# A graph-attention kernel: no repeated blocks at the ends of the spans, k and q[dst] in one PSUM tile, one load of edge features a step

## The chip, the cores and the metric

The kernel runs on one core of one Trainium2 chip. The metric is device microseconds (us) of one execution; the time before is the median of ten runs. TensorE is called PE in the profile, VectorE DVE, ScalarE ACT, GpSimd POOL and SyncE SP.

## The reference, cut to what matters

One layer of graph attention over N = 12500 nodes and E = 212500 edges of F = 128 features, with 8 heads of 16. The edges come sorted by their destination `dst`.

```python
h  = relu(layernorm(x))
q  = h @ Wq.T + bq;   v = h @ Wv.T + bv          # per node
k  = edge_attr @ Wk.T + bk                        # per edge
in_m, out_m, diag_m = sum16(q[src]*k), sum16(q[dst]*k), sum16(q[src]*q[dst])   # 8 heads each
score = (segsoftmax(in_m/4, dst) + segsoftmax(out_m/4, dst) + segsoftmax(diag_m/4, dst)) * edge_weight
out = x + leaky_relu(segsum(score * v[dst], dst) @ Wo.T + bo, 0.1)
```

So each edge has 24 logits, a softmax runs over all edges that end in one node, and two sums per node (the denominators and the weighted numerators) are all that goes back to the nodes.

## The kernel before, in words

All of the work is in `ordered_path`; `general_path` is skipped by a branch for these inputs.

**Blocks, spans and steps.** The edges are cut into NB = 416 blocks of BE = 512 (the last has EL = 20 edges). There are S = 5 spans of G = 83 blocks, and 5 x 83 + 1 = 416. A step t works on block t of each span, and there are T = G + 1 = 84 steps, so g = 5 t + s runs over 420 blocks: step 83 does the first block of spans 1 to 4 a second time (it needs their first edges, because a node's edges may reach over the end of a span), and the block of 20 edges, whose rest is filled with zeros.

**Preparation** (to about 130 us): weights and biases are turned, q of all nodes is computed and written to `q_table` (fp32) and `q3_table` (three bf16 terms), the sorted destinations become `rel_d` (place of the edge's node in its block) and `far_d` (minus 1e30 where a new node begins). The first LOOK = 9 blocks are gathered on POOL, and AHEAD = 6 blocks of edge features are loaded.

**The work on one block g**, by helper:

- `gather(g)` (L647): four indirect DMAs on POOL, 128 rows of q[src] each, into `qq[:, :, 0, :]`; the pool `gath` has QQ = 11 buffers of 4 KB per partition. Gather j of block g + LOOK also waits for a product of iteration g on PE (`behind`), which is a pacing rule only.
- `fetch_edges(g)` (L636): one 256 KB load of the block's edge features on the SP queue, six blocks ahead.
- `turn(g)` (L1100): four PE transposes of the features into PSUM `eT_ps` (L1103), copied by ACT to `eT` (L1105).
- `one_hots(g)` (L1092): two ACT passes (L1097, L1098) that make the one-hot matrix `oh` of the block's destinations.
- `spread_q(g)` (L1118): four PE products of `oh` with the window of q rows give q[dst] in PSUM `qd_ps` (2 buffers; L1122); ACT copies it to `qq[:, :, 1, :]` (L1124).
- `project(g)` (L1109): the bias (L1111) and four fp32 products `eT` x `wk` (L1113) give k in PSUM `k_ps` (2 buffers).
- `logits(g)` (L1128): on DVE the 512-wide product q[src] * q[dst] (L1133), the 1024-wide product of both halves of `qq` with k (L1134) and the reduction to 24 logits (L1136) in `lT`.

**The work on a step**, spread over the five iterations of later steps: `turn_logits` (l_ps, L1149) and `scan_on` at s = 0, `scan_back` at s = 1, `turn_max` (m_ps, L1175) and `powers` (L1181, exp L1182) at s = 2, `show_ends` (d_ps L1203, sel L1206, L1207) and `weigh_powers` (L1189) at s = 3, `to_rows` (w_ps L1216, rows L1221) and `put_rows` (five small stores) at s = 4. `fetch(t + 2)` and `fetch_rows(t + 2)` load `relb`, `far` and `win` on SP at s = 3. `nodes_before` and `nodes_between` do the finished nodes, four tiles every second step: two h passes each at s = 2 and 3 on ACT (L1014), two transposes and copies `hT` (L1034, L1037), the products with wv and wo (L1040, L1042), a slope pass (L1061), maximum and sum (L1066, L1067), and the store (L1073). Nodes at the ends of spans (`rest`) wait for the end: their sums come back by `ends_ab` loads (L1004 on SP, L1006 on the ACT queue), then scores, products and stores.

**The order is written by hand.** `pin` chains the instructions of each engine (and each DMA queue) in the order in which the code issues them. In the main loop (L1309) iteration g issues

```python
spread_q(g + 1); project(g + 1); turn(g + 2); logits(g); one_hots(g + 3)
# then the step's helper of this s, then nodes_between
```

so ACT's order in one iteration is: copy of q[dst] (g+1), copy of eT (g+2), the two one-hot passes (g+3), then what the step and the nodes need; PE's is: spread (g+1), bias and products (g+1), transposes (g+2), then the step's products.

Of the kernel before, what the change touches and what calls it, by code (L numbers as in the profile page):

```python
# [17 lines left out]
DIM = 16  # L18
# [454 lines left out]
def ordered_path(ctx: ExitStack, tc: tile.TileContext, flag, x, src, dst, edge_attr, edge_weight,  # L473
# [108 lines left out]
    LOOK, QQ, AHEAD, EA = 9, 11, 6, 7  # L582
# [28 lines left out]
    def fetch(t):  # L611

        if t >= T:
            return
        at, part = block_rows(t)
        relb = load.tile([K3, S, BE], BF, name="relb")
        pin(nc.sync.dma_start(relb, rel_d[part].rearrange("(s b) e -> s b e", b=G)
                              [None, :, at, :].to_broadcast([K3, S, BE])))
        far = load.tile([R, BE + 1], BF, name="far", bufs=4)
        for s in range(S):  # L620
            lo = (s * G + t) * BE
            pin(nc.sync.dma_start(far[s * H3:(s + 1) * H3, :],
                                  far_d[None, lo:lo + BE + 1].to_broadcast([H3, BE + 1])))
        _, base_v[t] = nc.values_load_multi_w_load_instructions(
            bases[0:1, t, 0:S], engines=[mybir.EngineType.SP], min_val=0, max_val=N - 1,
            skip_runtime_bounds_check_because="the indices of nodes are below N")
        st[t] = dict(relb=relb, far=far)

    def fetch_rows(t):
        if t >= T:  # L630
            return
        win = st[t]["win"] = load.tile([K3, S, F], BF, name="win")
        for s in range(S):
            pin(nc.sync.dma_start(win[:, s, :], q3_table[bass.ds(base_v[t][s] * 3, K3), :]))

    def fetch_edges(g):  # L636
        if g < S * T:
            ea = load.tile([P, JN * F], F32, name="ea", bufs=EA)
            b0 = (g % S * G + g // S) * BE
            n = min(BE, E - b0)  # L640
            if n < BE:
                nc.vector.memset(ea, 0.0)
            pin(nc.sync.dma_start(ea[:n // JN, :],
                                  edge_attr[b0:b0 + n, :].rearrange("(p j) f -> p (j f)", j=JN)))
            eas[g] = ea

    def gather(g):  # L647
        if g < S * T:
            qq = gath.tile([P, JN, 2, F], F32, name="qq")
            for j in range(JN):  # L650
                rows = pin(nc.gpsimd.indirect_dma_start(  # L651
                    out=qq[:, j, 0, :], out_offset=None, in_=q_table,
                    in_offset=bass.IndirectOffsetOnAxis(
                        ap=src_i[:, g % S * G + g // S, j:j + 1], axis=0)))
                if (g - LOOK, j) in behind:
                    tc.add_manual_dep(rows.ins, behind[g - LOOK, j], mybir.DependencyInfo(
                        mybir.DependencyClass.Sync, mybir.DependencyReason.SCHED_ONLY),
                        reason="close behind the products")
            qqs[g] = qq

# [14 lines left out]
    with tc.tile_pool(name="prep", bufs=1) as prep, \  # L675
# [234 lines left out]
        for g in range(-2, GN):  # L910
            if g + 2 < GN:
                rectify(g + 2)
            if 0 <= g + 1 < GN:
                turn_h(g + 1)
            if g >= 0:
                nodes_q(g)
            ready(g + 4)
            measure(g + 6 + min(max(g, 0), 6))
            if g in side:
                side[g]()  # L920
            if 9 <= g < 9 + AHEAD:
                fetch_edges(g - 9)
        for g in range(LOOK):
            gather(g)
        edges_4()
# [160 lines left out]
    with tc.tile_pool(name="work", bufs=2) as work, \  # L1086
            tc.tile_pool(name="scan", bufs=2) as scan, \
            tc.tile_pool(name="ps", bufs=1, space=PSUM) as ps:
        ks, eTs, qds, ohs, lTs = {}, {}, {}, {}, {}
        end = S * T  # L1090
# [9 lines left out]
        def turn(g):  # L1100
            eT_ps = ps.tile([P, JN, P], F32, name="eT_ps", bufs=1)
            for j in range(JN):
                pin(nc.tensor.transpose(eT_ps[:, j, :], eas[g][:, j * F:(j + 1) * F], ident))  # L1103
            eT = work.tile([P, JN, P], F32, name="eT", bufs=3)
            pin(nc.scalar.copy(eT, eT_ps))  # L1105
            eTs[g] = eT
            del eas[g]

        def project(g):  # L1109
            k_ps = ps.tile([P, JN, F], F32, name="k_ps", bufs=2)  # L1110
            pin(nc.tensor.matmul(k_ps, ones3, bk3, start=True, stop=False))  # L1111
            for j in range(JN):
                pin(nc.tensor.matmul(k_ps[:, j, :], eTs[g][:, j, :], wk, start=False,  # L1113
                                     stop=(j == JN - 1)))
            ks[g] = k_ps
            del eTs[g]

        def spread_q(g):  # L1118
            s, d = g % S, st[g // S]
            qd_ps = ps.tile([P, JN, F], F32, name="qd_ps", bufs=2)  # L1120
            for j in range(JN):
                pin(nc.tensor.matmul(qd_ps[:, j, :], ohs[g][:, j * P:(j + 1) * P],  # L1122
                                     d["win"][:, s, :], start=(j == 0), stop=(j == JN - 1)))
            pin(nc.scalar.copy(qqs[g][:, :, 1, :], qd_ps))  # L1124
            qds[g] = qd_ps
            del ohs[g]

        def logits(g):  # L1128
            s, t = g % S, g // S
            if s == 0:  # L1130
                lTs[t] = scan.tile([P, JN, S, H3], F32, name="lT", bufs=4)
            prod = work.tile([P, JN, 3, F], F32, name="prod")
            pin(nc.vector.tensor_mul(prod[:, :, 2, :], qqs[g][:, :, 0, :], qds[g]))  # L1133
            pin(nc.vector.tensor_mul(prod[:, :, 0:2, :], qqs[g],  # L1134
                                     ks[g][:, :, None, :].to_broadcast([P, JN, 2, F])))
# [3 lines left out]
            del ks[g], qds[g], qqs[g]  # L1139
# [5 lines left out]

        def turn_logits(t):
            l_ps = small([R, P, JN], "l_ps")
            for j in range(JN):
                pin(nc.tensor.transpose(l_ps[:, :, j], lTs[t][:, j].rearrange("p s c -> p (s c)"),  # L1149
                                        ident))  # L1150
            st[t]["l"] = l_ps

        def scan_on(t):
            d = st[t]
            u = d["u"] = scan.tile([R, BE], F32, name="u", bufs=3)
            pin(nc.vector.tensor_tensor_scan(u, d["far"][:, :BE], d["l"].rearrange("r p j -> r (p j)"),  # L1156
# [7 lines left out]
        def scan_back(t):  # L1164
            d = st[t]
            m = d["m"] = scan.tile([R, BE], F32, name="m")
            pin(nc.vector.tensor_tensor_scan(m[:, ::-1], d["far"][:, BE:0:-1], d["u"][:, ::-1],  # L1167
                                             d["head"][:, 0:1] if t < T - 1 else -FAR,
                                             op0=ALU.add, op1=ALU.max))

        def turn_max(t):
            d = st[t]
            m_ps = d["mT"] = small([P, JN, R], "m_ps")
            for j in range(JN):
                pin(nc.tensor.transpose(m_ps[:, j, :], d["m"][:, j:BE:JN], ident[:R, :R]))  # L1175

        def powers(t):
            d = st[t]
            back = d["back"] = work.tile([P, JN, S, 2, H3], F32, name="back")
            e = back[:, :, :, 0, :]  # L1180
            pin(nc.vector.tensor_sub(e, lTs[t], d["mT"].rearrange("p j (s c) -> p j s c", s=S)))  # L1181
            pin(nc.scalar.activation(e, e, AF.Exp, scale=SCALE))  # L1182
            del lTs[t]

        def weigh_powers(t):
# [3 lines left out]
            pin(nc.vector.tensor_mul(back[:, :, :, 1, :], back[:, :, :, 0, :],  # L1189
                                     att.to_broadcast([P, JN, S, H3])))  # L1190
# [20 lines left out]
        def to_rows(t):  # L1211
            d = st[t]
            w_ps = small([3 * W, 2, 3, 2 * H3], "w_ps")
            for i, (lo, _) in enumerate(trios):
                for j in range(JN):
                    pin(nc.tensor.matmul(w_ps[:, i].rearrange("p s c -> p (s c)"),  # L1216
                                         d["sel"][:, j, lo:lo + 3, :].rearrange("p s w -> p (s w)"),
                                         d["back"][:, j, lo:lo + 3].rearrange("p s i c -> p (s i c)"),
# [53 lines left out]
        starts, holds = (0, 1, 3, 4, 6), ("eT_ps", "k_ps", "k_ps", "qd_ps", "qd_ps")  # L1272
# [3 lines left out]
        def spare():  # L1276
            return gath.tile([P, JN, 2, F], F32, name="qq").rearrange("p j i f -> p (j i f)")

        def halves():
            return spare().rearrange("p (i j f) -> i p j f", i=2, j=JN)  # L1280

        def begin_rest(at):
            if at in turned:
                late.update(zip(turned[at], halves()))
            for r, (of, begin) in enumerate(zip(rest, starts)):
# [8 lines left out]
                if at == LOOK + (3, 4, 7, 7, 7)[r]:  # L1294
                    of.held = ps.tile([P, JN, F], F32, name=holds[r], bufs=1 if r == 0 else 2)
# [13 lines left out]
        for g in range(end + 2 * S):  # L1309
            s, t = g % S, g // S  # L1310
            nodes_before(t, s)
            if g < end:
                gather(g + LOOK)
                fetch_edges(g + AHEAD)
# [10 lines left out]
            one_hots(g + 3)  # L1325
            if s == 0:
                later(turn_logits, t - 1)
                later(scan_on, t - 1)
                later(select, t - 2)
            elif s == 1:  # L1330
                later(scan_back, t - 2)
            elif s == 2:
                later(turn_max, t - 2)
                later(powers, t - 2)
            elif s == 3:
                later(show_ends, t - 2)
                later(weigh_powers, t - 2)
                fetch(t + 2)
                fetch_rows(t + 2)
            else:  # L1340
                later(to_rows, t - 2)
                later(put_rows, t - 2)
# [71 lines left out]
```

## Time and profile before

| what | value |
|---|---|
| median of 10 runs | 2323.13 us (2318.01 to 2326.63) |
| the profiled execution | 2319.08 us; span of its instructions 2317.2 us |
| mean granted TensorE clock | 0.786 |
| busy: DVE, PE, POOL, ACT | 1985.5, 1694.5, 1678.4, 1356.2 us (86, 73, 72, 59% of the span) |
| indirect DMAs on POOL | 1680, busy 1636.4 us, idle just before them 524.3 us |
| first and last of them start at | 82.0 and 2234.6 us |

Times in rows are microseconds from the start of the span, unless ns is written. Busy time of an engine counts what the profile shows of its instructions; the gap between two instructions of an engine is its idle time, put down to what ended it. The granted clock is the share of full speed that TensorE was given.

### The profile page before, as it was taken

The page shows a single profiled execution, that of the slowest core. Times are in us where ns is not written, and L with a number is a line of the kernel's source. Part 1 is how long each engine was busy: PE and PEld are TensorE (multiplying, and loading weights), DVE is VectorE, ACT ScalarE, POOL GpSimd, SP SyncE. Part 2 cuts the span into 40 slices and gives each one's busy share as a digit, 9 for nine tenths or more (in the row PEclk, how much of TensorE's full clock was granted, in tenths as well). Part 3 has the DMA queues.
Part 4 walks back from the last instruction along what each step waited for, and adds up shares of the span by engine and source line. Part 5 has one row for each costly group of instructions (what it writes and reads, how often), then busy time and mean ns, then how long its engine had stood idle before and what let it go on. Part 6 is the DMA issues. An engine that isn't in the chain of part 4 may idle for free.

```text
span 2317.2 us, 36525 instructions
## 1 busy us (share of the span) xinstructions
PE 1694.5 (73%) x10293; PEld 1350.2 (58%) x10293; DVE 1985.5 (86%) x2191; ACT 1356.2 (59%) x2462; POOL 1678.4 (72%) x1717
## 2 busy tenths in 40 slices
PE   6348878767777777777777877777787877677783
PEld 4236666555656566566556655656665656565562
DVE  7669999888888888888889898988888888898973
ACT  6647666556555656565656665665656556565651
POOL 4577777777777777777777777777777777777741
PEclk9658887777777778877877797787778779788876
DMA  6885555555455545554555565455545555565521
GB/s 198 265 255 171 170 164 142 152 144 145 130 149 161 148 135 162 152 151 131 162 158 143 145 171 148 134 155 156 147 139 169 146 149 142 144 169 142 164 57 54
DMA packets 326673, 354.48 MB, mean 153 GB/s; under 512 B 143655, under 2 KB 245376, under 8 KB 326152
## 3 DMA queue, kind: packets, MB, share of 16 engines
q1 hardware_dynamic: 257117, 235.44, 34.9%
q0 software_dynamic: 53920, 110.41, 18.2%
q10 hardware_dynamic: 15424, 6.19, 1.1%
q8 instruction: 85, 1.39, 0.2%
q14 instruction: 127, 1.04, 0.2%
HBM read 319.65 MB, written 32.17 MB: 152 GB/s over the span
## 4 chain that ended last, share of the span: by engine, by line
DMA 33%; PE 29%; DVE 17%; issue 11%; ACT 5%; POOL 4%; DVEq 0%; SPq 0%; POOLq 0%; ACTq 0%
DMA qq<-q_table,src_i 30%; PE k_ps L1113 10%; DVE prod L1134 6%; PE w_ps L1216 5%; POOL qq L651 4%; DVE prod L1133 4%; PE eT_ps L1103 4%; PE k_ps L1111 3%; PE node_ps L1042 2%; PE qd_ps L1122 1%; DMA q_table<-q 1%; ACT eT L1105 1%; ACT relb L1097 1%; PE d_ps L1203 1%; DVE u L1156 1%
## 5 line engine op out<-in xcount | busy, mean ns | idle before, releaser
L651 POOL DMA_INDIRECT qq<-q_table,src_i x1680 | 1636.4, 974 | 524.3 <-issue 242.0
L1136 DVE TENSOR_REDUCE lT<-prod 128x96 f32<-128x1536 f32 x420 | 736.2, 1753 | 14.3
L1113 PEld LDWEIGHTS k_ps<-wk,eT 128*128 128x128 f32 x3360 | 522.1, 237 | 292.0 <-issue 85.6
L1113 PE MATMUL k_ps<-wk,eT 128*128 128x128 f32 x3360 | 617.5, 340 | 14.3 <-ACT eT L1105 13.9
L1134 DVE TENSOR_TENSOR prod<-qq,k_ps 128x1024 f32<-128x1024 f32 x420 | 509.9, 1214 | 2.0 <-PE k_ps L1113 2.0
L1133 DVE TENSOR_TENSOR prod<-qq,qd_ps 128x512 f32<-128x512 f32 x420 | 286.6, 682 | 222.7 <-DMA qq<-q_table,src_i 187.2
L1105 ACT COPY eT<-eT_ps 128x512 f32<-128x512 f32 x420 | 245.9, 585 | 388.5 <-PE eT_ps L1103 369.4
L1122 PE MATMUL qd_ps<-win,oh 126*128 126x128 bf16 x1680 | 184.2, 239 | 319.9 <-DVE prod L1133 252.2
L1122 PEld LDWEIGHTS <-oh 126*128 126x128 bf16 x1680 | 143.5, 107 | 378.6 <-issue 302.4
L1103 PE MATMUL eT_ps<-ident,ea 128*128 128x128 f32 x1680 | 319.9, 325 | 1.0 <-DVE found L937 1.0
L1097 ACT ACTIVATE relb<-relb,before 126x512 bf16<-126x512 bf16 x420 | 304.4, 725 | 0.0
L1111 PE MATMUL k_ps<-b,ones 3*128 3x512 bf16 x420 | 185.2, 441 | 143.5 <-DVE prod L1134 142.5
L1098 ACT ACTIVATE oh<-relb 126x512 bf16<-126x512 bf16 x420 | 264.6, 630 | 18.8 <-issue 5.4
L1124 ACT COPY qq<-qd_ps 128x512 f32<-128x512 f32 x420 | 241.5, 575 | 49.1 <-PE qd_ps L1122 22.3
L1182 ACT ACTIVATE back<-back 128x480 f32<-128x480 f32 x84 | 50.7, 604 | 362.9 <-DVE back L1181 350.7
L1103 PEld LDWEIGHTS eT_ps<-ident,ea 128*128 128x128 f32 x1680 | 256.5, 173 | 1.3 <-DVE found L937 1.3
L1216 PE MATMUL w_ps<-back,sel 128*126 128x144 f32 x1344 | 215.4, 322 | 19.6 <-ACT sel L1207 10.0
L1216 PEld LDWEIGHTS w_ps<-back,sel 128*126 128x126 f32 x1344 | 207.3, 224 | 26.2 <-ACT sel L1207 21.8
L1175 PE MATMUL m_ps<-ident,m 120*128 120x120 f32 x336 | 72.3, 351 | 58.5 <-DVE m L1167 58.4
L1156 DVE TENSOR_TENSOR_SCAN u<-far,u,l_ps 120x512 f32<-120x512 bf16 x83 | 105.5, 1271 | 1.3 <-PE l_ps L1149 1.3
L1167 DVE TENSOR_TENSOR_SCAN m<-far,head,u 120x512 f32<-120x512 bf16 x83 | 105.9, 1276 | 0.0
L1175 PEld LDWEIGHTS m_ps<-ident,m 120*128 120x128 f32 x336 | 54.6, 217 | 75.9 <-DVE m L1167 72.4
(167 smaller groups left out, 1292.6 us busy)
## 6 DMA issues: line engine op xcount, KB each, us to landing
ea<-in_edge_attr_dram SPq DMA_DIRECT2D x419, 256.0 KB
relb<-rel_d SPq DMA_DIRECT2D x84, 630.0 KB
qq<-q_table,src_i POOLq DMA_INDIRECT x1680
win<-q_table SPq DMA_DIRECT2D x420, 31.5 KB
far<-far_d SPq DMA_DIRECT2D x420, 24.0 KB
q_table<-q SPq DMA_DIRECT2D x24, 384.0 KB
sums<-rows SPq DMA_DIRECT2D x412, 7.9 KB
q_table<-xq SPq DMA_DIRECT2D x24, 256.0 KB
```

The lines of the kernel that those rows point to most:

```text
L651: rows = pin(nc.gpsimd.indirect_dma_start(out=qq[:, j, 0, :], out_offset=None, in_=q_table, in_offset=bass.IndirectOffsetOnAxis(ap=src_i[: ...
L1097: pin(nc.scalar.activation(d, d, AF.Abs, bias=before[:K3]))
L1098: pin(nc.scalar.activation(oh, d, AF.Relu, bias=1.0, scale=-1.0))
L1103: pin(nc.tensor.transpose(eT_ps[:, j, :], eas[g][:, j * F:(j + 1) * F], ident))
L1105: pin(nc.scalar.copy(eT, eT_ps))
L1111: pin(nc.tensor.matmul(k_ps, ones3, bk3, start=True, stop=False))
L1113: pin(nc.tensor.matmul(k_ps[:, j, :], eTs[g][:, j, :], wk, start=False, stop=(j == JN - 1)))
L1122: pin(nc.tensor.matmul(qd_ps[:, j, :], ohs[g][:, j * P:(j + 1) * P], d["win"][:, s, :], start=(j == 0), stop=(j == JN - 1)))
L1133: pin(nc.vector.tensor_mul(prod[:, :, 2, :], qqs[g][:, :, 0, :], qds[g]))
L1134: pin(nc.vector.tensor_mul(prod[:, :, 0:2, :], qqs[g], ks[g][:, :, None, :].to_broadcast([P, JN, 2, F])))
L1136: pin(nc.vector.tensor_reduce(lTs[t][:, :, s, :], prod.rearrange("p j i (h d) -> p j (i h) d", d=DIM), AX.X, ALU.add))
L1216: pin(nc.tensor.matmul(w_ps[:, i].rearrange("p s c -> p (s c)"), d["sel"][:, j, lo:lo + 3, :].rearrange("p s w -> p (s w)"), d["back"][:, ...
```

## The change

- `end` becomes S * G = 415: the repeated blocks are not gathered, transposed or multiplied any more. The first 64 logits of each span's first block (`l_few`) are kept in `l_end` at step 1, moved up by one span with a small DMA; the 20 last edges are done once, as single edges, by `logits_few` in iteration s = 1 of step 1. Step 83 is left as a short one: scan, difference, exp and sums over 64 edges a span. It is done in the same five iterations as steps 81 and 82 (`now`), all after the last block.
- `qq` holds q[src] alone (2 KB per partition, 19 buffers), LOOK is 12. k and q[dst] get one PSUM tile `kq_ps` of two banks (2 buffers, as many banks as before); ACT copies its q[dst] half to a tile `qd` of its own. DVE multiplies q[src] with both halves (1024 wide), then `qd` with k (512 wide).
- `fetch_edges(t)` loads the features of a whole step (1.25 MB) into one of 2 buffers, one step ahead. `far` comes in one DMA instead of five.
- The loop has one iteration more after the blocks, and the tiles that `rest` borrows are named anew.

```diff
-    LOOK, QQ, AHEAD, EA = 9, 11, 6, 7
+    LOOK, QQ = 12, 19
+    end = S * G
...
-        for s in range(S):
-            lo = (s * G + t) * BE
-            pin(nc.sync.dma_start(far[s * H3:(s + 1) * H3, :],
-                                  far_d[None, lo:lo + BE + 1].to_broadcast([H3, BE + 1])))
+        lo = t * BE
+        of = bass.AP(far_d.tensor, far_d.offset + lo, [[G * BE, S], [0, H3], [1, BE + 1]])
+        pin(nc.sync.dma_start(far, of))
...
+    def fetch_edges(t):
+        if t < G:
+            ea = eas[t] = load.tile([P, S, JN * F], F32, name="ea")
+            pin(nc.sync.dma_start(
+                ea, edge_attr[:end * BE, :].rearrange("(s b p j) f -> p s b (j f)", s=S, b=G, p=P)
+                [:, :, t, :]))
...
         def project(g):
-            k_ps = ps.tile([P, JN, F], F32, name="k_ps", bufs=2)
+            k_ps = kqs[g][:, 0]
             pin(nc.tensor.matmul(k_ps, ones3, bk3, start=True, stop=False))
...
         def spread_q(g):
             s, d = g % S, st[g // S]
-            qd_ps = ps.tile([P, JN, F], F32, name="qd_ps", bufs=2)
+            kqs[g] = ps.tile([P, 2, JN, F], F32, name="kq_ps", bufs=2)
+            qd_ps = kqs[g][:, 1]
             for j in range(JN):
                 pin(nc.tensor.matmul(qd_ps[:, j, :], ohs[g][:, j * P:(j + 1) * P],
                                      d["win"][:, s, :], start=(j == 0), stop=(j == JN - 1)))
-            pin(nc.scalar.copy(qqs[g][:, :, 1, :], qd_ps))
-            qds[g] = qd_ps
+            qds[g] = work.tile([P, JN, F], F32, name="qd")
+            pin(nc.scalar.copy(qds[g], qd_ps))
...
-            pin(nc.vector.tensor_mul(prod[:, :, 2, :], qqs[g][:, :, 0, :], qds[g]))
-            pin(nc.vector.tensor_mul(prod[:, :, 0:2, :], qqs[g],
-                                     ks[g][:, :, None, :].to_broadcast([P, JN, 2, F])))
+            pin(nc.vector.tensor_mul(prod[:, :, 0:2, :],
+                                     qqs[g][:, :, None, :].to_broadcast([P, JN, 2, F]),
+                                     kqs[g].rearrange("p i j f -> p j i f")))
+            pin(nc.vector.tensor_mul(prod[:, :, 2, :], qds[g], kqs[g][:, 0]))
...
-        for g in range(end + 2 * S):
+        for g in range(end + 2 * S + 1):
...
+            now = [t - 2] if t < G else [G - 2, G - 1] if t == G else []
             if s == 0:
-                later(turn_logits, t - 1)
-                later(scan_on, t - 1)
-                later(select, t - 2)
+                if 0 < t <= G:
+                    turn_logits(t - 1)
+                    scan_on(t - 1)
+                if t == G:
+                    scan_on(G)
+                for i in now:
+                    later(select, i)
...
             else:
-                later(to_rows, t - 2)
-                later(put_rows, t - 2)
+                for i in now:
+                    later(to_rows, i)
+                    later(put_rows, i)
+                if t == G:
+                    for f in (select, turn_max, powers, show_ends, weigh_powers, to_rows, put_rows):
+                        f(G)
```

## The prediction

> **What bounds the kernel now.** I read the costliest groups first, then the gathers' own answer, then the timeline of one step. From the groups:
>
> ```profile
> L651 POOL DMA_INDIRECT qq<-q_table,src_i x1680 | 1636.4, 974 | 524.3 <-issue 242.0
> L1113 PE MATMUL k_ps<-wk,eT 128*128 128x128 f32 x3360 | 617.5, 340 | 14.3 <-ACT eT L1105 13.9
> L1105 ACT COPY eT<-eT_ps 128x512 f32<-128x512 f32 x420 | 245.9, 585 | 388.5 <-PE eT_ps L1103 369.4
> L1111 PE MATMUL k_ps<-b,ones 3*128 3x512 bf16 x420 | 185.2, 441 | 143.5 <-DVE prod L1134 142.5
> ```
>
> DVE has the largest busy share (86%), but POOL sets the pace: the gathers' busy and idle time is 2160.7 us, and 504 of the 524 idle are a constant 0.30 ahead of each of 1680. From 82.0 to 2235.5 us POOL does nothing else: 2153.5 / 84 = 25.64 us a step of 20 gathers. DVE, ACT and PE wait for gathers.
>
> What matters for this change is how PE and ACT hand a block to each other. Timeline, one slow and one fast pass of PE, with ACT between:
>
> ```profile
> 1008.65 0.59 PE L1122 MATMUL qd_ps<-win,oh 126*128 126x128 bf16 x4 [2.37 <-DVE prod L1133]
> ...
> 1009.78 0.58 PE L1111 MATMUL k_ps<-b,ones 3*128 3x512 bf16 x1 [0.55 <-DVE prod L1134]
> ...
> 1010.29 2.08 PE L1113 MATMUL k_ps<-wk,eT 128*128 128x128 f32 x8
> ...
> 1012.16 1.06 PE L1103 MATMUL eT_ps<-ident,ea 128*128 128x128 f32 x4
> 1013.26 0.59 ACT L1105 COPY eT<-eT_ps 128x512 f32<-128x512 f32 x1
> 1013.74 0.72 ACT L1097 ACTIVATE relb<-relb,before 126x512 bf16<-126x512 bf16 x1
> 1014.50 0.63 ACT L1098 ACTIVATE oh<-relb 126x512 bf16<-126x512 bf16 x1
> 1015.04 0.91 ACT L1206 ACTIVATE sel<-d_ps 128x420 f32<-128x420 f32 x2
> ...
> 1023.07 0.39 PE L1111 MATMUL k_ps<-b,ones 3*128 3x512 bf16 x1
> 1023.39 1.16 PE L1113 MATMUL k_ps<-wk,eT 128*128 128x128 f32 x8
> 1024.38 0.60 PE L1103 MATMUL eT_ps<-ident,ea 128*128 128x128 f32 x4
> ```
>
> From the start of the bias to the end of the transposes PE takes 3.44 us slow, 1.91 fast. ACT starts eT 0.04 after the transposes and reaches its next instruction 1.78 later (eT, relb, oh). Today these two lie beside each other: project(g+1) needs only the eT copied an iteration earlier.
>
> **The new wait.** In the changed program k and q[dst] are one tile, and the bias matmul of k(g+1) waits for ACT's copy of q[dst](g+1), issued just before it. Behind that matmul stand, in PE's order, the four products, the transposes of g+2 and the step's products; behind the transposes, ACT's eT, relb and oh, and behind these ACT's next copy of q[dst], for which the next bias waits. So PE and ACT take turns in one ring. A plain iteration: transposes end, 0.04, 1.78 of ACT, the copy 0.575 (its group's mean), 0.045 to PE (as from DVE to L1111), then PE: 2.44 + 3.44 = 5.88 slow, 2.44 + 1.91 = 4.35 fast.
>
> Work in the ring adds to the 2.44: s=1 one hT copy a step, 0.53: 2.97. s=2 exp 0.55, and two h passes every second step (0.43): 3.42. s=3 sel 1.80; in even steps two h passes and the slope (5.67), in odd ones wv's product before the next spread (4.80 slow, 4.24 fast): 5.23, 4.95. s=4 ACT's rows waits for w_ps, 3.12 or 2.12, then the spread and the copy: 4.37, 3.17. With s=0 that is 18.4 slow, 17.0 fast; five PE passes are 17.2 or 9.55. The step takes **35.6 us slow, 26.5 fast**, both above POOL's 25.64. The ring becomes the bound.
>
> **Which clock.** In the PE rows the short and long durations switch on a 3.41 us grid. From the main loop's rows: of 65 windows of 3.41 us in slow state with PE busy up to 80%, none turned fast, of 145 busy 100%, 57% did; in fast state busy up to 60%, 62 of 75 turned slow, above 75% almost none. By the pieces above the ring keeps PE about 86% busy when slow and 66% when fast, so it falls back often and recovers often; before it was fast for (0.786 - 0.5) / 0.5 = 57% of the time. I take 45%: 1 / (0.45/26.5 + 0.55/35.6) = 30.8 us a step.
>
> A rule against that: the Trainium skill, "TensorE: Matmul & The Clock Gate", Part 1, grants full clock after one busy window of about 3.4 us and takes it back only after an idle window of that length. The ring's gaps are at most 3.2 us, so by the rule it would stay fast, 26.5 a step, some 2440 us. The rows above show fast windows turning slow well before they are idle; I go by them.
>
> **The other parts, on the path or not.**
> - 20 gathers fewer, two of 20 rows more: 18 x 1.274 = 22.9 us of POOL; five blocks fewer of the rest. With the ring as the bound this is in the count of 83 steps.
> - LOOK 12: POOL's four waits at 139 to 176 us (5.1 together) go; worth 5.1 while POOL bounds, nothing here.
> - DVE: same widths, each product with one PSUM operand (1214 and 682 ns before). The 512-wide one now follows; spread(g+2) waits for it instead of for the first product. DVE needs 23 us a step, less than the ring; bounds -1 to +2 a step, 0 taken.
> - One 1.25 MB load: issued at s=0, needed by the transposes at s=3, 15 us later; at the 152 GB/s of the span it lands in 8.4. Hidden; without cover about 5 us a step, as an upper bound.
> - far: four issues fewer (0.4 us each) on SP, which waits 640 us for rows anyway: 0. The skill, "DMA: Bandwidth & Descriptors", on why a DMA increments its semaphore by 16, lets it run on 5 engines only (outer size 5), where 24 allowed 12. It is fetched two steps ahead and landed in 5.87 us; no cost either way.
> - Few: some twenty small instructions at step 1, PE waiting for ACT and DVE between: 0 to 10 us once, 3 taken.
> - The end: before, 74.3 us from the last logits (2242.9) to the span's end. Now steps 81 and 82 both come after the last block, and select of step 83 stands on SP behind ten stores: +6. ACT's and SP's ends_ab loads now stand behind the slope and store of the last pair, and PE does these after the rest's four products (5.9 us before): +9. Bounds 0 to 20, 15 taken.
>
> **Sum**, in the profiled execution: first bias 132.9, DMA waits at 150 to 173 us 12 (as ACT's rows show there), 83 x 30.8 = 2556, few 3, last logits 3.6, end 74.3 + 15, outside the span 1.9: 2799. The median lies 4 above the profiled execution: **2803 us**. Ring all fast: 83 x 26.5 gives 2446. All slow: 3201.
>
> **Rivals.**
> 1. The ring stays below the gathers (ACT's rows overlap more than I count): faster. Needs under 25.64 us a step. Then 2323 - 22.9 - 5.1 + 15 = 2310. For: today's ACT waits 369 us for the transposes, so it has slack. Against: even the fast count is 26.5. 10%; another 2% that it ends within 0.2%, about what a measurement of this kernel can tell from none.
> 2. The ring runs fast nearly always, 2446 to 2560. For: PE recovers at s=4, where it is busy for 7 us. Against: each fast iteration has 2 us of PE idle. 20%.
> 3. The ring at 28 to 33 us a step: 2570 to 2980. 60%.
> 4. Nearly always slow, 2980 to 3200: 8%. The late load of features, added to the ring, ends here too.
>
> Faster 0.10, same 0.02, slower 0.88. The range takes cases 2 and 3: 2440 to 2980; the likeliest case alone is 2570 to 2980.
>
> **What would show it.** The bias matmul waiting for the q[dst] copy some 1.8 us in nearly every block, PE and ACT in turn; POOL's gathers with idle gaps well over 0.30; DVE no more waiting for gathers but for k; granted clock near 0.7. Wrong if gathers stay back to back to the end, or if the bias still waits for DVE.

## The result, and the profile after

The changed kernel takes **2696.29 us** (median of 9 runs, 2682.07 to 2706.86) where the kernel before takes 2323.66. The ratio is 1.1606, with a 95% interval of 1.1588 to 1.1623: the time grew by 16%. The forecast was 2803, with a range of 2440 to 2980. The profiled execution took 2692.13 us; its span is 2690.3 and its mean granted clock 0.743 (before 0.786).

The same groups as in the prediction, from the changed kernel's profile (busy us, mean ns of one, then the idle time ahead and what ended it). In the changed code the gathers are L649, the bias is L1126, k's products are L1128, the copy of eT is L1121, and DVE's 1024-wide product is L1148:

```profile
L649 POOL DMA_INDIRECT qq<-q_table,src_i x1660 | 1609.7, 970 | 835.4 <-issue 340.2 <-PE kq_ps L1128 288.8 <-PE kq_ps L1137 130.0
L1128 PE MATMUL kq_ps<-wk,eT 128*128 128x128 f32 x3320 | 663.4, 362 | 0.0
L1121 ACT COPY eT<-eT_ps 128x512 f32<-128x512 f32 x415 | 243.2, 586 | 1130.3 <-PE eT_ps L1119 1130.3
L1126 PE MATMUL kq_ps<-b,ones 3*128 3x512 bf16 x415 | 184.2, 444 | 779.7 <-ACT qd L1140 777.7 <-ACT oh L1114 2.0
L1148 DVE TENSOR_TENSOR prod<-qq,kq_ps 128x1024 f32<-128x1024 f32 x415 | 503.7, 1214 | 269.1 <-PE kq_ps L1128 221.7 <-issue 38.1 <-DMA qq<-q_table,src_i 8.7
```

No operation of POOL, ACT or DVE in these rows got longer: a gather takes 970 ns (974 before), the copy of eT 586 (585). One of k's products takes 362 ns in the mean where it took 340, at the lower granted clock. What changed most is the idle column. The bias matmul, which had waited for DVE's second product, now waits for ACT's copy of q[dst] (L1140): 777.7 us in 414 waits, 1.88 us each. ACT's copy of eT waits 1130.3 us for the transposes (369.4 before). The gathers' idle time went from 524.3 to 835.4 us, and DVE's first product of a block now waits 221.7 us for k and 8.7 for gathers. Before, that first product was the 512-wide one, and it waited for gathers:

```profile
L1133 DVE TENSOR_TENSOR prod<-qq,qd_ps 128x512 f32<-128x512 f32 x420 | 286.6, 682 | 222.7 <-DMA qq<-q_table,src_i 187.2 <-ACT qq L1124 13.3 <-ACT relb L1097 11.8
```

The timeline of two passes, PE's matmuls and ACT alone, shows the two engines taking turns. PE turns slow within the first pass (its products take 1.85 us) and runs fast in the second (1.16):

```profile
1007.15 0.57 ACT L1140 COPY qd<-kq_ps 128x512 f32<-128x512 f32 x1
1007.77 0.37 PE L1126 MATMUL kq_ps<-b,ones 3*128 3x512 bf16 x1 [1.77 <-ACT qd L1140]
1008.07 1.85 PE L1128 MATMUL kq_ps<-wk,eT 128*128 128x128 f32 x8
1009.71 1.06 PE L1119 MATMUL eT_ps<-ident,ea 128*128 128x128 f32 x4
1010.56 0.63 PE L1137 MATMUL kq_ps<-win,oh 126*128 126x128 bf16 x4
1010.81 0.59 ACT L1121 COPY eT<-eT_ps 128x512 f32<-128x512 f32 x1 [3.09 <-PE eT_ps L1119]
1011.29 0.72 ACT L1113 ACTIVATE relb<-relb,before 126x512 bf16<-126x512 bf16 x1
1012.04 0.63 ACT L1114 ACTIVATE oh<-relb 126x512 bf16<-126x512 bf16 x1
1012.58 0.57 ACT L1140 COPY qd<-kq_ps 128x512 f32<-128x512 f32 x1
1013.20 0.37 PE L1126 MATMUL kq_ps<-b,ones 3*128 3x512 bf16 x1 [2.00 <-ACT qd L1140]
1013.50 1.16 PE L1128 MATMUL kq_ps<-wk,eT 128*128 128x128 f32 x8
1014.49 0.60 PE L1119 MATMUL eT_ps<-ident,ea 128*128 128x128 f32 x4
1014.93 0.64 PE L1225 MATMUL m_ps<-ident,m 120*128 120x120 f32 x4
1015.13 0.59 ACT L1121 COPY eT<-eT_ps 128x512 f32<-128x512 f32 x1 [1.98 <-PE eT_ps L1119]
```

The bias starts 0.05 after the copy ends, and ACT's eT starts 0.04 after the transposes end. The spread that fills the bank (L1137) had ended 1.39 us ahead of its copy: PE had long done its part, and the copy stood in ACT's order behind eT, relb and oh. From 136.0 to 2596.5 us there are 415 bias matmuls, so a step takes 5 x 2460.5 / 414 = **29.72 us**. Before, it took 25.64 by the gathers, and 25.03 by the 420 bias matmuls from 132.9 to 2230.3 us.

### The profile page after: what moved, and what is told of

It is laid out like the page before. It is cut to its first block, busy times and chain, and to the rows that moved or that the text cites. A ratio compares the mean times of both kernels' runs of the same rounds, so it can differ in the third digit from the quotient of the medians.

```text
span 2690.3 us, 34046 instructions
## 1 busy us (share of the span) xinstructions
PE 1785.9 (66%) x10209; PEld 1469.4 (55%) x10209; DVE 1975.4 (73%) x2179; ACT 1342.9 (50%) x2445; POOL 1653.4 (61%) x1699
## 5 line engine op out<-in xcount | busy, mean ns | idle before, releaser
L649 POOL DMA_INDIRECT qq<-q_table,src_i x1660 | 1609.7, 970 | 835.4 <-issue 340.2
L1128 PEld LDWEIGHTS kq_ps<-wk,eT 128*128 128x128 f32 x3320 | 560.6, 255 | 925.2 <-issue 925.2
L1121 ACT COPY eT<-eT_ps 128x512 f32<-128x512 f32 x415 | 243.2, 586 | 1130.3 <-PE eT_ps L1119 1130.3
L1126 PE MATMUL kq_ps<-b,ones 3*128 3x512 bf16 x415 | 184.2, 444 | 779.7 <-ACT qd L1140 777.7
L1148 DVE TENSOR_TENSOR prod<-qq,kq_ps 128x1024 f32<-128x1024 f32 x415 | 503.7, 1214 | 269.1 <-PE kq_ps L1128 221.7
L1128 PE MATMUL kq_ps<-wk,eT 128*128 128x128 f32 x3320 | 663.4, 362 | 0.0
L1151 DVE TENSOR_TENSOR prod<-qd,kq_ps 128x512 f32<-128x512 f32 x415 | 282.2, 680 | 0.0
L1273 PE MATMUL w_ps<-back,sel 128*126 128x144 f32 (+1 forms) x1344 | 245.3, 353 | 1.6 <-ACT sel L1263 1.6
L1273 PEld LDWEIGHTS w_ps<-back,sel 128*126 128x126 f32 (+1 forms) x1344 | 244.2, 258 | 2.4 <-ACT sel L1263 2.4
L1140 ACT COPY qd<-kq_ps 128x512 f32<-128x512 f32 x415 | 238.3, 574 | 1.4 <-PE kq_ps L1137 0.6
L1137 PE MATMUL kq_ps<-win,oh 126*128 126x128 bf16 x1660 | 193.1, 249 | 48.4 <-DMA win<-q_table 46.4
L1137 PEld LDWEIGHTS <-oh 126*128 126x128 bf16 x1660 | 150.3, 114 | 86.2 <-ACT oh L1114 49.2
L1262 ACT ACTIVATE sel<-d_ps 128x420 f32<-128x420 f32 x168 | 76.8, 508 | 8.4 <-PE d_ps L1259 8.4
```

The costliest lines, as they stand in the source:

```text
L649: rows = pin(nc.gpsimd.indirect_dma_start(out=qq[:, j, :], out_offset=None, in_=q_table, in_offset=bass.IndirectOffsetOnAxis(ap=src_i[:, g ...
L1140: pin(nc.scalar.copy(qds[g], qd_ps))
L1148: pin(nc.vector.tensor_mul(prod[:, :, 0:2, :], qqs[g][:, :, None, :].to_broadcast([P, JN, 2, F]), kqs[g].rearrange("p i j f -> p j i f")))
L1151: pin(nc.vector.tensor_mul(prod[:, :, 2, :], qds[g], kqs[g][:, 0]))
```

## The experiments

The kernels ran in groups, each group on one chip. On the chips of the first two groups the kernel before itself took 2723.91 and 2703.01 us instead of 2320, so those runs are read by their ratio to it alone, and not against the times in us that their expectations name; what their traces show of that is in the last section.

**The order turned round.** The tile stays shared; k is written ahead of q[dst].

```diff
         def project(g):
+            kqs[g] = ps.tile([P, 2, JN, F], F32, name="kq_ps", bufs=2)
...
         def spread_q(g):
-            kqs[g] = ps.tile([P, 2, JN, F], F32, name="kq_ps", bufs=2)
...
+                project(g + 1)
+                behind[g + 1, 0] = pinned[products]
                 spread_q(g + 1)
-                behind[g + 1, 0] = pinned[products]
-                project(g + 1)
```

> The changed kernel with one order turned round: project(g+1) is issued before spread_q(g+1), in the same shared tile. The bias matmul then writes a tile nobody has read yet and waits only for DVE's second product of the block two before, and ACT's copy of q[dst] waits for a product that stands behind k's in PE's order anyway. Theory (the ring of PE and ACT through the shared tile is the whole loss): the bias's 1.87 us wait for the copy goes, gathers bound again: 25.64 us a step, 83 steps, less 5 for LOOK, more 15 at the end: 2310 us, between 2290 and 2350. Rival 1 (the loss is in what the shared banks do to PE and ACT at work, or in the late load of features, or in the three reorderings of DVE): nothing changes, 2650 to 2720. Rival 2 (half of it is DVE's later product): about 2500.

Measured: 2700.75 us where the kernel before takes 2723.91, ratio 0.9915 (0.9898 to 0.9931). It was run again in a later group, on a chip where the kernel before takes 2319.03:

> The order turned round (project before spread_q, shared tile kept), beside the changed kernel and the kernel before on one chip. Theory: the whole loss goes, 0.98 to 1.00 of the kernel before. Rival (part of the loss stays): over 1.02.

Measured: 2308.80 us (median of 10, 2302.30 to 2315.14), ratio 0.9957 (0.9938 to 0.9976). Groups of that second run; the bias is L1127 here:

```profile
L649 POOL DMA_INDIRECT qq<-q_table,src_i x1660 | 1611.6, 971 | 512.9 <-issue 264.3 <-DMA qq<-q_table,src_i 113.1 <-PE kq_ps L1137 25.3
L1127 PE MATMUL kq_ps<-b,ones 3*128 3x512 bf16 x415 | 182.3, 439 | 458.4 <-DVE prod L1151 457.0 <-DVE prod L1148 0.6 <-issue 0.5
L1121 ACT COPY eT<-eT_ps 128x512 f32<-128x512 f32 x415 | 244.4, 589 | 29.0 <-PE eT_ps L1119 27.9
L1148 DVE TENSOR_TENSOR prod<-qq,kq_ps 128x1024 f32<-128x1024 f32 x415 | 504.5, 1216 | 196.9 <-DMA qq<-q_table,src_i 169.5 <-ACT qd L1140 10.0 <-ACT relb L1113 3.8
```

The wait for the copy is gone, the gathers are back to back again (512.9 / 1660 = 0.31 us between two), and DVE waits for gathers. The step is 25.5 us. With the order alone changed, the whole loss is gone, so neither the shared banks nor the step's load nor the order of DVE's products lengthens the run while the gathers set the pace. This version is also faster than the kernel before, by what is left of the rest of the change.

**Two tiles again.** The order stays as changed; k and q[dst] get a tile of one bank each, and DVE does three 512-wide products.

```diff
-            kqs[g] = ps.tile([P, 2, JN, F], F32, name="kq_ps", bufs=2)
-            qd_ps = kqs[g][:, 1]
+            qd_ps = ps.tile([P, JN, F], F32, name="qd_ps", bufs=2)
+            qps[g] = qd_ps
...
-            k_ps = kqs[g][:, 0]
+            k_ps = kqs[g] = ps.tile([P, JN, F], F32, name="k_ps", bufs=2)
```

> The changed kernel with k and q[dst] in two PSUM tiles of one bank each, as before the change, and the order as changed. DVE then does three 512-wide products (about 0.68 each, 2.04) where it did a 1024-wide and a 512-wide one (1.89): 0.7 us a step more of DVE, which has room below 25.64. Theory (ring through the shared tile): 2310 us, 2290 to 2360, the same as with the order turned round; a bias that waits for DVE or nothing. Rival (the order or the later load, not the tile): 2650 to 2720.

Measured: 2715.02 us against 2723.91, ratio 0.9962 (0.9948 to 0.9976), and in its trace the bias waits 77.2 us, nearly all of it put down to its issue (39.1) and to DVE (37.1). Either half of the pair undone, the tile or the order, removes the loss: it needs both.

**The shared tile alone**, in the kernel before.

```diff
-            qd_ps = ps.tile([P, JN, F], F32, name="qd_ps", bufs=2)
+            kqs[g] = ps.tile([P, 2, JN, F], F32, name="kq_ps", bufs=2)
+            qd_ps = kqs[g][:, 1]
...
-            k_ps = ps.tile([P, JN, F], F32, name="k_ps", bufs=2)
+            k_ps = kqs[g][:, 0]
```

> The kernel before with one part of the change alone: k and q[dst] in one PSUM tile of two banks, 2 buffers, order and everything else as before (repeated blocks gathered, 84 steps, one load a block). Theory: the same ring; its pieces in the changed kernel's trace give 29.7 us a step, 132.9 + 12 + 84 x 29.7 + 3.6 + 74 + 2 = 2720 us, 2680 to 2760, and a bias that waits about 1.9 us for the copy. Rival (the loss comes with the dropped blocks, the step's load or the deeper look-ahead): 2323.

Measured: 3152.50 us against 2723.91, ratio 1.1564 (1.1525 to 1.1604); the theory's 2720 / 2323 is 1.171, the rival's 1. Its bias group:

```profile
L1111 PE MATMUL kq_ps<-b,ones 3*128 3x512 bf16 x420 | 203.5, 485 | 1091.4 <-ACT qq L1125 934.8 <-issue 97.5 <-ACT back L1183 24.9
```

One part of the change, put into the old kernel with nothing else, gives a loss of the same size (1.156 here, 1.161 for the whole change) and the same wait: 1091.4 / 420 = 2.6 us for each bias on this chip, 934.8 of the 1091.4 put down to the copy.

**Doses.** ACT's work inside the ring is lengthened, taken out, or left in with the ring gone; and PE is kept busier.

```diff
+            pin(nc.scalar.copy(qds[g], qd_ps))        # copy done twice
...
+            one_hots(g + 3)                           # one-hot passes ahead of turn
             turn(g + 2)
             logits(g)
-            one_hots(g + 3)
...
-            for j in range(JN):                       # products that spread q, four times
+            for j in list(range(JN)) * (4 if s else 1):
```

> The changed kernel with its shared tile and its false wait, but the two one-hot passes of ACT (0.72 and 0.63, issue to issue 1.29) issued ahead of turn(g+2): ACT's order is copy of q[dst], relb, oh, eT, so that the passes lie beside PE's products and transposes and leave the ring. Theory: each iteration loses 1.29 us as long as PE's pass is longer than that (3.44 slow, 1.91 fast): 29.7 - 6.4 = 23.3 us a step, below the gathers' 25.64, which bound again with some slow stretches above them: 2300 to 2420, 2340 taken. Rival (not a ring: PE waits for something else that the copy only happens to end with): 2650 to 2720.

> The changed kernel with ACT's copy of q[dst] done twice, the second onto the same tile. The next bias then waits for the second copy. Theory (ring): each of 415 iterations gets 0.53 us longer (0.574 less the overlap of two ACT instructions), 220 us, and the PE, idle for longer, some more of the slow clock: 1.25 to 1.29 of the kernel before (2900 to 3000 where that takes 2323). Rival (no ring: ACT, busy 50% of the span, has room for it): 1.16, as without the second copy.

> The order turned round (project before spread_q, shared tile kept) and the copy of q[dst] done twice as well. Theory: with the false wait gone ACT's copies are off the path, so the second copy costs nothing: 0.98 to 1.00 of the kernel before, and the bias waits only for DVE. Rival (the copy holds up DVE's product or PE in another way, or ACT is short of time): 1.03 to 1.10.

> The changed kernel with the four products that spread q done four times over for four blocks of five (all but s = 0), each time with the same result: 1.17 us more of PE at the fast clock, put where PE waits for ACT's copy, to see what the clock alone is worth. If fast windows that are busy under about 60% are what turns the clock down, the share of slow windows falls and the step goes from 29.7 towards the all-fast ring of 26.5, less what the added products put on the path (about 1.2 us in half the steps, after wv's product): 1.05 to 1.10 of the kernel before. Rival (the clock is not decided by the busy share of single windows, or the ring does not care): the added products cost their part on the path, 1.16 to 1.20.

> The one-hot passes ahead of turn(g+2) once more, beside the doses above on one chip. Theory (ring): 1.29 us less in each iteration, the gathers bound again but for stretches at the slow clock: 0.99 to 1.05 of the kernel before. If the gain stops at 1.04 again, what is late is to be read from which wait of the ring is left: the bias for the copy in iterations s = 3 and 4, where sel, rows and w_ps stay in the ring. Rival (no ring): 1.16.

Measured: one-hots earlier 1.0411 (1.0363 to 1.0459) and again 1.0464 (1.0443 to 1.0485); the copy twice 1.1537 (1.1518 to 1.1557); the copy twice with the order turned round 0.9944 (0.9927 to 0.9960); the products four times 1.1411 (1.1392 to 1.1430). The second copy on the turned order costs nothing, as expected. Of the three versions with the ring, the earlier one-hots came out at the upper end of what was expected (about 1.04, then 0.99 to 1.05). The copy twice missed 1.25 to 1.29 and stands where its rival had put it (1.16), and the products four times fell between their theory (1.05 to 1.10) and their rival (1.16 to 1.20). These totals decide nothing by themselves, since the changed kernel had no run on those two chips, and 1.16 need not be its ratio there. Two controls on a third chip (the second was shown above), and the kernel before for its trace:

> The changed kernel itself, as the control for the doses: the kernel before took 2700 to 2724 in the two groups of runs so far, where it had taken 2323, so its ratio there need not be 1.16. The ring's length is set by ACT and PE durations that are the same in all traces (copy 0.575, products 1.16 or 2.08). Theory (ring): about 2900, that is 1.07 of the kernel before, with the second copy's 3117 some 215 above it and the earlier one-hots' 2829 below it. Rival (the ratio 1.16 holds everywhere, 3130): then the second copy cost nothing, and the ring does not bound here.

> The kernel before, for a profile of it under the conditions of these runs. If the engines' durations are those of the first profile (gather 0.97, product 1.21, copy 0.59) and the extra 380 us are idle time, the column to read is which engine's semaphore arrives late: in the trace with the order turned round, ACT's copy of q[dst] starts up to 6 us after the products it needs have ended, at the time at which PE's semaphore is recorded. Theory: the same here, PE's semaphores late. Rival: longer gathers or a lower granted clock.

That chip gave the first times again: the changed kernel 2698.93 us, ratio 1.1636 (1.1591 to 1.1680), the kernel before 2323.45. So neither the expectation of 2900 for the control nor that of late semaphores for the kernel before was put to the test, and the doses needed a trace that holds its own control. The last kernel has all of them beside each other:

```diff
+        def part(g):
+            return min(g // S // 17, 4)      # 0 as changed, 1 one-hots, 2 copy twice, 3 order, 4 products
```

> The changed kernel in five parts, to have the doses beside each other in one trace, whatever the chip: steps 0 to 16 as changed; 17 to 33 with the one-hot passes ahead of turn(g+2); 34 to 50 with the copy of q[dst] done twice; 51 to 67 with project ahead of spread_q; 68 to 82 with the products that spread q done four times over in the blocks with s > 0. Read from the starts of the bias matmuls, as us a step. On a chip where the kernel before takes 2320, theory (ring, and the clock by the busy share of windows): 29.7; 23.3 by the ring, so the gathers' 25.6 to 26.5; 29.7 + 5 x 0.53 = 32.4 and some slow clock, 32.4 to 34; 25.6; 27 to 29. Rival to the ring: five equal parts near 29.7. Rival to the clock's share: 31 to 34 in the last part, where the added products lie on the path. On a chip where the kernel before takes 2700, the same order of the parts, each some 1 to 4 us longer.

It ran where the kernel before takes 2324.20. Windows of its trace, one for each part, its first three steps left out (busy time of PE, PE's weight loads, DVE, ACT and POOL; granted clock; DMA share; GB/s):

```profile
227.00:645.00 418.00, 282.55 (x1555) 233.33 (x1554) 300.72 (x280) 199.03 (x351) 271.75 (x282) 0.72 0.41 122
728.00:1115.00 387.00, 272.89 (x1658) 217.56 (x1658) 315.97 (x318) 216.37 (x380) 271.76 (x282) 0.82 0.47 139
1216.00:1678.00 462.00, 297.35 (x1681) 246.10 (x1680) 317.92 (x317) 251.66 (x449) 271.29 (x279) 0.76 0.38 116
1745.00:2063.00 318.00, 253.02 (x1662) 203.57 (x1662) 313.70 (x318) 213.87 (x382) 242.73 (x248) 0.85 0.55 162
2151.00:2500.00 349.00, 256.38 (x2000) 221.14 (x2000) 263.52 (x267) 187.01 (x339) 218.79 (x227) 0.83 0.42 124
```

The first four windows are 14 steps each, the last 11.8. From the starts of the bias matmuls, us a step:

| part | step | expected | plain iteration, fast clock |
|---|---|---|---|
| as changed | 29.83 | 29.7 | 4.32 |
| one-hots earlier | 27.64 | 25.6 to 26.5 | 3.23 |
| copy twice | 32.97 | 32.4 to 34 | 4.94 |
| order turned round | 22.75 | 25.6 | 2.51 |
| products four times | 29.55 | 27 to 29 | 4.33 |

- The second copy adds 0.62 us to every plain iteration and 3.1 to a step, on an engine that is busy 50% of the span. With the order turned round it added nothing. That is the ring.
- The one-hot passes taken out shorten the plain iteration by 1.09, but the step by 2.2 where 5 x 1.29 was reckoned. Waits of ACT in that part's window:

```profile
ACT eT L1124 <- PE eT_ps L1122: 82.1, 70, 2.2
ACT back L1241 <- DVE back L1240: 48.2, 14, 3.4
ACT rows L1285 <- PE w_ps L1280: 28.1, 14, 2.9
```

  In the shorter ring ACT reaches exp (L1241) before DVE has its input ready, and waits 48.2 / 14 = 3.4 us in each step (1.3 us in all in the first part's window). Behind it stands the copy of q[dst], so that wait is in the ring: DVE became its third member. The expectation had left DVE out.
- The turned order runs at 22.75, below the gathers' 25.6, and can only for a while: POOL did 248 gathers in a window whose 14 steps use 280, living on the twelve blocks gathered ahead. DVE is busy for 313.7 of 318 us there. Behind the gathers, DVE is the next bound.
- The products done four times raised the clock (0.83; 0.79 in the same steps of the first trace of the changed kernel) and left the step at 29.55 (29.66 there), above the 27 to 29 expected. What the clock gave, the added products took: PE's passes, from the bias to the end of the transposes, add up to 11.65 us a step (12.68 there), and the rest of the ring to 18.04 (17.10 there).

## Why the prediction was right, and where a term was off

**The ring: right.** The bias waits for the copy 1.88 us (forecast some 1.8) in nearly every block, POOL's gaps are 835.4 / 1660 = 0.50 instead of 0.31, DVE waits for k, the clock is 0.743. Undoing the tile or the order removes it, the tile alone brings it, a dose of ACT's time lengthens it.

**The rest of the change: right.** The sum of rival 1, for a kernel with no ring, was 2310; with the order turned round 2308.80 was measured, at 25.5 us a step. The load of a whole step is hidden: the transposes of the changed kernel's trace never wait for it. The end took 86.0 us from the last logits (2604.3) to the span's end, where 74.3 + 15 was reckoned: +11.6.

**The step: 30.8 forecast, 29.72 measured.** 83 x 1.08 = 90 of the 107 us that the forecast was too high. The waits at 150 to 173 us (12) and the few (3) also came out small: the first three steps take 30.9 each, 3.5 us more than three mean steps. An iteration can be parted at the end of its transposes; measured from the changed kernel's trace, and for the forecast from its pieces (30.8 is a mix of 53% of the fast step and 47% of the slow one):

| us a step | forecast fast, slow | forecast at 30.8 | measured |
|---|---|---|---|
| PE's passes, bias to end of transposes | 9.55, 17.2 | 13.2 | 13.2 |
| the rest, to the next bias | 17.0, 18.4 | 17.6 | 16.5 |

The passes came out as forecast. The term that was mis-sized is the rest, by the whole 1.1 us, and in it the work for the finished nodes. The prediction counts an hT copy in every step and h passes, slope and wv's product in every second. The kernel before has far fewer of them in its 84 steps:

```profile
L1014 ACT ACTIVATE h<-x_in,shift,inv 128x128 f32<-128x128 f32 x80 | 34.5, 478 | 0.0
L1037 ACT COPY hT<-node_ps 128x512 f32<-128x512 f32 x40 | 22.7, 567 | 0.0
L1061 ACT ACTIVATE h<-node_ps 128x512 f32<-128x512 f32 x20 | 11.5, 577 | 2.0 <-PE node_ps L1042 2.0
```

Four of the 80 h passes (L1014) belong to a group of four tiles, so there are 20 groups, one in about every fourth step and not in every second as the description of the kernel has it. Without this work the rest is right to 0.1: 2.43 us at s = 1, 2.92 at s = 2, 4.18 to 4.3 at s = 3.

| iteration | rest forecast fast, slow | rest measured | whole iteration | PE's clock at its start and end |
|---|---|---|---|---|
| s = 0 | 2.44 | 2.46 | 4.41 | fast at both in 80 of 83 |
| s = 1 | 2.97 | 2.72 | 5.12 | fast at both in 64, turns slow in 17 |
| s = 2 | 3.42 | 3.20 | 5.50 | fast at both in 38, turns slow in 27 |
| s = 3 | 4.95, 5.23 | 4.47 | 7.63 | slow at both in 41, turns slow in 33 |
| s = 4 | 3.17, 4.37 | 3.68 | 7.09 | slow at its start, fast at its end in 73 |

A plain iteration came out at 4.33 fast and 5.88 slow (two of s = 0 that were slow throughout), to 0.02 of the forecast.

**The share of the clock: near, by judgement.** The 45% fast was taken and not worked out; 49% was measured between the first and the last bias, so part of that agreement is luck. PE was busy 56% in fast windows and 80% in slow ones, where 66 and 86 were reckoned. The counts of windows are off too: by the granted clock of the kernel before's main loop (133 to 2235 us), 0 of 85 slow windows busy up to 80% turned fast, 87 of 118 (74%) at 100%, and 86 of 107 fast windows busy up to 60% turned slow. They point the same way. Nor is there one clock for a whole step: it mostly turns slow in s = 1 to 3, and comes back during s = 4, where PE does the 16 products for w_ps.

**What the clock is worth in the ring, an estimate.** With every pass at the fast 1.91 us the measured step would be 16.5 + 9.55 = 26.1, close to the 25.5 of the turned order. By that, most of the loss is slow clock that the ring exposes: in the kernel before PE was slow for 43% of the span too, but there the gathers set the pace. No run shows the ring at the full clock.

**The rule on the clock: the rows decided rightly.** The Trainium skill, "TensorE: Matmul & The Clock Gate", Part 1, takes the full clock back after an idle window of about 3.4 us. By it the ring would have stayed fast, which the prediction's pieces put at an estimated 2440 or so. The trace disagrees: of 122 windows of 3.41 us between 150 and 2190 us after which the granted clock fell, none was idle throughout; the longest gap of PE inside one was 3.13 us, the median 1.87. Some gaps of the ring were longer than the 3.2 us of the prediction, up to 3.8, but only 21 were longer than 3.41, while the clock fell 145 times in the main loop.

## What to carry to other kernels

In these programs two halves of one tile were one thing to whatever orders reads and writes: a copy out of one half made the next write to the other half wait, and the writer's engine with all that stood behind it. When tiles are merged, let every producer write before the first consumer reads; here the same tile cost 16% in one order and nothing in the other. And an engine that is half idle can still be the bound: look for a chain of waits that closes on itself, and test it by adding work to the idle member.

## What the runs showed of the hardware

**When the clock turns.** These are counts in the traces of two kernels, not a rule. By the granted clock of the changed kernel's trace, in windows of 3.41 us between 150 and 2190 us: a fast window with PE busy below 50% was followed by a slow one 106 times of 112, between 50 and 60% 16 times of 44, above 60% never (133); from 136 to 2596 us it was once in 165, and in the kernel before's trace, between 150 and 2190 us, 4 times of 45 between 60 and 70% and never above (202). A slow window with PE busy below 70% was followed by a fast one never (92), between 80 and 99% 24 times of 64, at 99% or more 97 times of 114.

**Two chips on which the kernel before took 380 to 400 us more.** The kernel before has no trace from there. In the trace of the turned order the engines' durations are the same (a gather 0.98, the 1024-wide product 1.21, the reduction 1.75). The kernel before had a granted clock of 0.75 to 0.76 there (0.78 to 0.81 elsewhere). Waits of ACT with the order turned round, first on such a chip, then on the other:

```profile
ACT qd L1140 <- remote: 362.6, 87, 7.8
ACT eT L1121 <- remote: 172.2, 95, 3.7
ACT qd L1140 <- PE kq_ps L1137: 110.7, 86, 3.5
```

```profile
ACT qd L1140 <- PE kq_ps L1137: 417.7, 256, 8.2
ACT back L1234 <- DVE back L1233: 293.6, 81, 8.2
ACT rows L1278 <- PE w_ps L1273: 32.6, 32, 4.9
```

"remote" is an update that the trace can't place: it has lost many of the semaphore records there. By those that it kept, the copy of q[dst] started over 0.3 us after its products, DVE's reading and ACT's own last work had all ended in 207 of 412 blocks, by up to 6.7 us, and in 202 of them within 0.15 us (median 0.02) after an update of PE's semaphore; on the other such chip, with the copy done twice, in 189, and 188 of them so. On the chip where the kernel before takes 2319.03 the turned order's copy was late in 4 blocks. The first update recorded after four products of L1137 comes 0.87 us later in the median there (an upper bound, since records are lost) and 0.01 later in the trace of the turned order on the other chip. So PE's updates come late on those two chips; why they do was not found. Where two of the versions ran on more than one chip, their order was the same.
